# A graph-network layer: hand-overs between the engines used a step later, and the edge filter's bias added by a product

## The chip, the cores and the metric

The kernel runs on one core of one Trainium2 chip. The metric is the device time of one launch in microseconds (us); nine runs of the kernel before had a median of 5747.03 us (5734.28 to 5781.86). The core's engines each work through a queue of their own in order: TensorE (PE, with its weight loads listed as PEld), VectorE (DVE), ScalarE (ACT), GpSimd (POOL, which here issues the indirect transfers) and SyncE (SP, which issues the other transfers). They wait for one another by semaphores.

## The reference

```python
h = relu(layernorm(x))                      # 12500 nodes x 128
h = h @ W_in2f
Wij = ssp(f_ij @ W_f1 + b_f1) @ W_f2 + b_f2 # 412500 edges, f_ij has 20 columns
Wij = Wij * rcut_ij[:, None]
x_ij = h[idx_j] * Wij                       # idx_j = dst, sorted
agg = segment_sum(x_ij, idx_i)              # idx_i = src, in no order
out = x + ssp(agg @ W_o1 + b_o1) @ W_o2 + b_o2
```

`ssp` is softplus less log 2. All is in float32. The rows of `h` are gathered by the sorted index, so 512 edges after one another need few different rows; the sums go to the unsorted index.

## The kernel before

**Chunks.** The edges are cut into 806 chunks of 512 (four tiles of 128), four chunks to a group, and the groups into seven segments. For each chunk: PE makes the hidden layer `z` (L653) for a pair of chunks at a time; ACT takes |z|, Exp and Ln of it (L656, L657, L662) and DVE joins them to `r` (L668). PE multiplies `r` by W_f2 into `v` (L764), one fp32 product per tile, on top of the bias.

**The bias.** The two biases of the hidden layer and of the filter are joined once to `bf12`, the same row on all 128 partitions (`biases`, L304). For the first two chunks PE writes it into `v` by a product of one row of ones; for the others ACT copies it there (L757), and the products then add to it.

**Picking.** DVE makes a one-hot matrix `at` of a chunk's node numbers (L744), SP loads 32 rows of `h`, split in three bf16 parts, into `near` (L608), and PE's products of the two, one per tile, give the gathered rows `picked` (L772). ACT scales them by the edge weight to `hg` (L780). `v` and `picked` share three PSUM banks by the tag "v".

**Message and scatter.** DVE multiplies `v` by `hg` into `o` (L791); POOL scatters the four tiles of `o` to slots in DRAM by indirect transfers (L795).

**Slots.** To know the slots, DVE marks each edge's block of 128 source nodes (`inb`, L673), PE adds running counts in the bank `free` (L725 and L692), and DVE takes the count that belongs to each edge by a maximum, `top` (L697). From four chunks' `top` it makes slot numbers (L717 to L721), in the first group for each chunk alone.

**Collecting.** When a segment's edges are all scattered, SP reads its slots back to `m`, DVE makes a one-hot `to` of the node within the block (L844), and PE's products `acc` (L857) sum the rows, added into `agg` (L878, L880). This runs under the chunks of the next segments; the last segment is collected after the last chunk, together with the layer's end (`finish`).

**Order.** The order on each engine is written out by hand: `step(k)` issues the work around chunk k, and what a step issues stands in each engine's queue in that order. Before, step k issues on DVE `inb`, in even steps `r`, `at` for chunk k+2, then the message `o` of chunk k, the sum into `agg`, `to`, and last `top` of the count that PE makes in the same step. On PE it issues `value` for k+1, `pick` for k+1, the two count products, in even steps `z` of k+4, and the collecting products. On ACT: the bias copy for k+2, `hg` for k+1, Abs and Exp of k+4 or, in odd steps, Ln.

Of the kernel before, what the change touches and what calls it, by code (L numbers as in the profile page):

```python
# [9 lines left out]
F32 = mybir.dt.float32  # L10
BF16 = mybir.dt.bfloat16
# [6 lines left out]
P = 128  # L18
# [23 lines left out]
def gnn_kernel(  # L42
# [107 lines left out]
    turn = sbuf("turn", [P, NCHUNK, QT])  # L150
    places = sbuf("places", [P, P])
    bf12 = sbuf("bf12", [P, P])
    zero = sbuf("zero", [P, ZR * RW])
    bad = sbuf("bad", [1, NFLAG])
    none = sbuf("none", [P, 3 * P], BF16)
# [96 lines left out]
    def constants():  # L252

        early[0] = load_x(0)
        part_load(0)
        first_load(0)
        nc.sync.dma_start(win, w_in2f)

        for j in range(NCHUNK):
            nc.sync.dma_start(wf1[32 * j:32 * j + RBF, :], w_f1)  # L260

        nc.scalar.preload_act_table_set("natural_log_exp_and_others")
        nc.scalar.dma_start(bf1, b_f1[:, None])
        nc.scalar.dma_start(wf2, w_f2)
        nc.scalar.dma_start(bf2, b_f2[None, :].to_broadcast([P, P]))
        make_identity(nc, ident)
        for _ in bounds(0, nc.gpsimd):
            pass

        prow_i = early_room[:WP, rows_at + 5 * NC:rows_at + 5 * NC + 1].bitcast(I32)  # L270
        nc.gpsimd.iota(prow_i, pattern=[[0, 1]], base=0, channel_multiplier=43)
        nc.gpsimd.iota(places, pattern=[[1, P]], base=0, channel_multiplier=0,
                       allow_small_or_imprecise_dtypes=True)

        nc.gpsimd.memset(after, 1.0)
        nc.gpsimd.affine_select(out=after, in_=after, compare_op=ALU.is_ge, fill=0.0, base=-1,
                                pattern=[[1, P]], channel_multiplier=-1)
        nc.gpsimd.memset(zero, 0.0)

        nc.gpsimd.memset(before, 1.0)  # L280
        nc.gpsimd.affine_select(out=before, in_=before, compare_op=ALU.is_ge, fill=0.0, base=-1,
                                pattern=[[-1, P]], channel_multiplier=1)
        nc.gpsimd.iota(spare, pattern=[[1, 1]], base=N, channel_multiplier=1,
                       allow_small_or_imprecise_dtypes=True)
        nc.vector.memset(eps, EPS)
        nc.vector.memset(half, 0.5)
        nc.vector.memset(bad, 0.0)
        nc.vector.memset(rel[:, NPART - 1, :], 0.0)
        nc.vector.memset(ones, 1.0)
        nc.vector.memset(none, 0.0)  # L290

        for t in range(QT):
            nc.vector.memset(turn[:, :, t:t + 1], -1.0 if t % 2 else 1.0)
        nc.vector.tensor_scalar(prow_i, prow_i, 7, None, op0=ALU.logical_shift_right)
        nc.vector.tensor_copy(prow, prow_i)
        nc.vector.scalar_tensor_tensor(after, ident, BIG, after, op0=ALU.mult, op1=ALU.add)

        nc.vector.tensor_scalar(rest_of, after, -1.0, 1.0, op0=ALU.mult, op1=ALU.add)

    def biases(psum):  # L300

        nc.vector.tensor_scalar(nbf1, bf1, -1.0, None, op0=ALU.mult)
        b12 = psum.tile([P, QT, P], F32, name="b12", tag="acc")[:, 0, :]
        nc.tensor.matmul(b12, bf1.to_broadcast([P, P]), wf2, start=True, stop=True)  # L304
        nc.vector.tensor_add(bf12, b12, bf2)

    def late_loads():
        nc.sync.dma_start(wo1, w_o1)
# [85 lines left out]
        nc.scalar.activation(a, a, AF.Exp, scale=-1.0)  # L394
        nc.scalar.activation(a, a, AF.Ln, bias=half, scale=0.5)

    def finish(t0, n, sT, quad, psum):


        n0 = t0 * P  # L400
# [21 lines left out]
            xi = xo[:p, cs, :]  # L422
            nc.vector.tensor_add(xi, xi, spread(bo2[:p, :], xi.shape[1]))
        yield
        v = psum.tile([P, QT, P], F32, name="v_out", tag="v", bufs=3)
        for i in range(n):
            nc.tensor.matmul(v[:, i, :], r_n[:, i * P:(i + 1) * P], wo2, start=True, stop=True)
        yield
# [89 lines left out]
    with tc.tile_pool(name="edge", bufs=2) as edge, tc.tile_pool(  # L518
# [46 lines left out]
        class Group:  # L565
# [82 lines left out]
            def hidden(self, c):  # L648

                z = psum.tile([P, 2, CH], F32, name="z")  # L650
                for k in range(2):
                    rows = slice(32 * (c + k), 32 * (c + k) + RBF)
                    nc.tensor.matmul(z[:, k, :], wf1[rows, :], self.f[rows, :],  # L653
                                     start=True, stop=True)
                a = quad.tile([P, 2, CH], F32, name="a", bufs=2)
                nc.scalar.activation(a, z, AF.Abs, bias=bf1)  # L656
                nc.scalar.activation(a, a, AF.Exp, scale=-1.0)  # L657
                self.pair[c] = z, a

            def hidden_log(self, c):  # L660
                _, a = self.pair[c]
                nc.scalar.activation(a, a, AF.Ln, bias=half, scale=0.5)  # L662

            def hidden_end(self, c):

# [30 lines left out]
            def rank_end(self, c):  # L696
# [3 lines left out]
                if self.g * NCHUNK + c == seg.c1 - 1:  # L700
# [7 lines left out]
                    for b0, b1 in ((0, seg.b0), (seg.b0, seg.b1), (seg.b1, NBLK)):  # L708
                        i += 1
                        if b0 < b1:  # L710
                            self.limit(i + 1, ALU.is_gt, seg.tiles(b0) * P // 2,
                                       both[:, :, 0, b0:b1])
                if c == self.n - 1 or self.g == 0:

                    w = slice(c * QT if self.g == 0 else 0, (c + 1) * QT)
                    top = self.top[:, w]
                    nc.vector.scalar_tensor_tensor(top, top, -BIG,  # L717
                                                   turn.rearrange("p c t -> p (c t)")[:, w],
# [26 lines left out]
                                        op=ALU.is_equal)  # L745
                self.at_w = at

            def bias(self, c):


                v = psum.tile([P, QT, P], F32, name="v", bufs=3)
                if self.g * NCHUNK + c < 2:
                    nc.tensor.matmul(v.rearrange("p t f -> p (t f)"),
                                     ones[0:1, :].to_broadcast([1, P]), spread(bf12[0:1, :], QT),
                                     start=True, stop=False, skip_group_check=True)
                else:
                    nc.scalar.activation(v, spread(bf12, QT), AF.Copy)  # L757
                return v

            def value(self, c, v):  # L760

                r = self.pair[c // 2 * 2][:, c % 2, :]
                for i in range(QT):
                    nc.tensor.matmul(v[:, i, :], r[:, i * P:(i + 1) * P], wf2,  # L764
                                     start=False, stop=True, skip_group_check=True)
                return v

            def pick(self, c, at, ps):

                near = self.near.pop(c)  # L770
                for i in range(QT):
                    nc.tensor.matmul(ps[:, i, :], at[:, i * P:(i + 1) * P], near,  # L772
                                     start=i == 0, stop=i == QT - 1, skip_group_check=True)

            def picked(self, c, ps):

# [111 lines left out]
        def of(k):  # L888
            return groups[k // NCHUNK], k % NCHUNK

        hgs, ats, vs, bs = {}, {}, {}, {}

        summed = []
        owed = []
# [29 lines left out]
        def window(g, c):  # L924
            g.window(c)
            ats[g.g * NCHUNK + c] = g.at_w

        def group(j):
            if j not in groups and j < NG:
                groups[j] = Group(j)  # L930
# [9 lines left out]
        def step(k, units=()):  # L940

            def has(j):
                return 0 <= j < NCH

            group((k + LG) // NCHUNK)
            part("rows", min(k + LW, 2 * k + 3, NEXT if k < NEXT - 3 else NCH), rows)
            for c, u in units:
                c.load(u + AHEAD)  # L950

            part("blocks", min(k + LR + 1, 2 * k + 1), blocks)
            part("end", min(k + LZ - 2, made.get("log", -1)), pairs(hidden_end))
            part("window", k + 2 if k > 0 else k + 1, window)
            if has(k):
                g, c = of(k)
                g.message(c, vs.pop(k), hgs.pop(k))
            for c in owed:
                c.keep()
            owed.clear()  # L960
            if has(k + 1):
                g, c = of(k + 1)
                vs[k + 1] = g.value(c, bs.pop(k + 1))
                ps = psum.tile([P, QT, P], F32, name="picked", tag="v", bufs=3)
                g.pick(c, ats.pop(k + 1), ps)
            if has(k + 2):

                bs[k + 2] = of(k + 2)[0].bias(of(k + 2)[1])
            if has(k + 1):
                hgs[k + 1] = g.picked(c, ps)  # L970
            for c, u in units:
                c.compare(u)
            upto = max(made["rank"], min(k + LR, 2 * k + 1))
            ready = [ranks(j) for j in range(made["rank"] + 1, upto + 1)]
            made["rank"] = upto
            for r in ready[:1]:
                next(r, None)
            part("hidden", k + LZ, pairs(hidden))
            part("log", k + LZ - 1, pairs(hidden_log))
            for c, u in units:  # L980
                if summed:
                    summed[0].add(summed[1])
                summed[:] = c, u
            for r in ready:
                for _ in r:
                    pass

        zeros = {}
        units = {}
# [79 lines left out]
        with tc.manual_schedule():  # L1069
# [21 lines left out]
            part("rows", 1, rows)  # L1091
            biases(psum)
            part("end", 0, hidden_end)
            bs[0] = groups[0].bias(0)
            group(1)
            aside = side()
            for k in range(-1, max(NCH, max(units) + 1)):
# [22 lines left out]
            for b in range(0, NBLK, QT):  # L1120
                n = min(QT, NBLK - b)
                sT = kept["agg"][:, b:b + n, :].rearrange("p c f -> p (c f)")
                outs.append(finish(b, n, sT, quad, psum))

            def go(q):
                if 0 <= q < NQ:
# [85 lines left out]
```

## Time and profile before

| | |
|---|---|
| median of 9 runs | 5747.03 us |
| profiled execution | 5746.84 us |
| its span | 5745.1 us, 71871 instructions |
| mean granted TensorE clock | 0.721 of full |
| busy: PE, DVE, POOL, ACT | 67%, 59%, 54%, 47% |
| first scatter issued | 29.4 us after the start |
| DMA, mean over the span | 143 GB/s |

The profile is one execution. A group of instructions has its line, engine, operation, the names of what it writes and reads, its count, then its busy time and the mean length of one in ns, then the time that its engine stood idle just ahead of it and who ended most of that. "Issue" means that nothing in the profile explains the wait. fp32 products appear as two records each.

### The profile page before, as it was taken

How to read it: one execution, taken by the hardware profiler on the slowest of the kernel's cores; microseconds unless marked ns; L12 is line 12 of the kernel's file. 1: busy time of each engine (PE TensorE's matmuls, PEld its weight loads, DVE VectorE, ACT ScalarE, POOL GpSimd, SP SyncE). 2: the span in 40 equal slices, each digit the busy share in tenths (PEclk: the TensorE clock that was granted, in tenths of full speed). 3: DMA queues.
4: the chain of work that ended last, by engine and by line, in shares of the span. 5: the costliest groups of instructions: out<-in, count | busy, mean ns of one | idle time of the engine just before them, and what ended most of it. 6: DMA issues, size and time to landing. Idle time of an engine off the chain costs nothing. (4 is left out here: it accounts for less than half of the span.)

```text
span 5745.1 us, 71871 instructions
## 1 busy us (share of the span) xinstructions
PE 3848.1 (67%) x21576; PEld 2895.6 (50%) x21576; DVE 3380.4 (59%) x6726; ACT 2718.1 (47%) x5490; POOL 3101.0 (54%) x3244
## 2 busy tenths in 40 slices
PE   6555555555555555477777777777777777777668
PEld 3333333333333333356656566656666665656557
DVE  5555555555444444456665666666666666666667
ACT  4555454555444444444444444444444444444444
POOL 5555555555555555555555555555555555555550
PEclk7666566666565565678877777787787777777889
DMA  5444444343333333255664554655555556545447
GB/s 151 138 135 142 130 126 133 116 132 106 101 90 91 100 106 93 81 147 162 184 192 139 155 157 146 192 166 162 151 170 183 160 151 181 168 141 148 141 131 219
DMA packets 515581, 820.80 MB, mean 143 GB/s; under 512 B 177074, under 2 KB 312870, under 8 KB 515186
## 3 DMA queue, kind: packets, MB, share of 16 engines
q1 hardware_dynamic: 411586, 602.85, 36.9%
q0 software_dynamic: 103168, 213.15, 11.3%
q8 instruction: 176, 2.88, 0.2%
q14 instruction: 219, 1.79, 0.1%
q10 hardware_dynamic: 432, 0.13, 0.0%
HBM read 419.09 MB, written 396.64 MB: 142 GB/s over the span
## 5 line engine op out<-in xcount | busy, mean ns | idle before, releaser
L795 POOL DMA_INDIRECT slots<-o,slot x3224 | 3097.9, 961 | 2503.6 <-DVE o L791 1600.4
L764 PE MATMUL v<-wf,r 128*128 128x128 f32 x6448 | 1203.6, 345 | 539.2 <-issue 229.3
L857 PEld LDWEIGHTS acc<-to,m 128*128 128x128 f32 x8132 | 1232.2, 235 | 579.1 <-issue 311.7
L857 PE MATMUL acc<-to,m 128*128 128x128 f32 x8132 | 1324.6, 326 | 281.2 <-DVE agg L880 133.9
L764 PEld LDWEIGHTS v<-wf,r 128*128 128x128 f32 x6448 | 1079.3, 252 | 847.4 <-issue 335.4
L780 ACT ACTIVATE hg<-picked,rcut 128x128 f32<-128x128 f32 x3224 | 913.3, 365 | 1213.3 <-remote 835.7
L697 DVE TENSOR_REDUCE top<-free 128x4 f32<-128x392 f32 x806 | 451.9, 561 | 1587.8 <-remote 942.8
L757 ACT ACTIVATE v<-bf 128x512 f32<-128x512 f32 x804 | 478.1, 595 | 1230.4 <-DVE o L791 902.7
L653 PE MATMUL z<-f,wf 20*128 20x512 f32 x1612 | 654.7, 867 | 404.2 <-DVE r L668 241.3
L844 DVE TENSOR_TENSOR to<-count_ps,m 128x512 f32<-128x512 f32 (+3 forms) x824 | 644.5, 806 | 281.3 <-remote 98.0
L772 PE MATMUL picked<-near,at 96*128 96x128 bf16 x3224 | 398.4, 256 | 470.5 <-ACT hg L780 273.0
L668 DVE SCALAR_TENSOR_TENSOR r<-z,nbf,a 128x1024 f32<-128x1024 f32 x403 | 516.3, 1281 | 238.7 <-ACT a L662 124.8
L656 ACT ACTIVATE a<-z,bf 128x1024 f32<-128x1024 f32 x403 | 454.0, 1127 | 403.7 <-remote 294.5
L772 PEld LDWEIGHTS <-at 96*128 96x128 bf16 x3224 | 313.4, 118 | 533.1 <-issue 506.1
L791 DVE TENSOR_TENSOR o<-v,hg 128x512 f32<-128x512 f32 x806 | 548.5, 680 | 15.5 <-ACT hg L780 8.7
L744 DVE TENSOR_TENSOR at<-count_ps,rel 96x512 bf16<-96x512 f32 x806 | 545.8, 677 | 0.0
L653 PEld LDWEIGHTS z<-f,wf 20*128 20x128 f32 x1612 | 173.8, 238 | 620.7 <-issue 381.9
L662 ACT ACTIVATE a<-a,half 128x1024 f32<-128x1024 f32 x403 | 468.1, 1162 | 0.0
L673 DVE TENSOR_TENSOR inb<-count_ps,blk 128x392 f16<-128x392 f32 x806 | 446.5, 555 | 0.0
L657 ACT ACTIVATE a<-a 128x1024 f32<-128x1024 f32 x403 | 426.2, 1057 | 12.8
L725 PE MATMUL free<-inb,rest_of 128*128 128x392 f16 x806 | 334.9, 416 | 129.3 <-issue 47.9
L692 PE MATMUL free<-inb,after 128*128 128x392 f16 x806 | 335.3, 416 | 17.6 <-issue 12.6
(108 smaller groups left out, 1145.5 us busy)
## 6 DMA issues: line engine op xcount, KB each, us to landing
m<-slots SPq DMA_DIRECT2D x311, 387.0 KB
m<-slots SPq DMA_DIRECT2D x317, 258.0 KB
rel<-rel_d SPq DMA_DIRECT2D x202, 384.0 KB
m<-slots SPq DMA_DIRECT2D x172, 322.5 KB
slots<-o,slot POOLq DMA_INDIRECT x3224
slots<-zero SPq DMA_DIRECT2D x96, 387.0 KB
slots<-zero SPq DMA_DIRECT2D x64, 516.0 KB
f<-in_f_t SPq DMA_DIRECT2D x404, 80.0 KB
```

Source lines behind the costliest of these rows:

```text
L653: nc.tensor.matmul(z[:, k, :], wf1[rows, :], self.f[rows, :], start=True, stop=True)
L662: nc.scalar.activation(a, a, AF.Ln, bias=half, scale=0.5)
L668: nc.vector.scalar_tensor_tensor(r, z, nbf1, a, op0=ALU.max, op1=ALU.add)
L744: nc.vector.tensor_tensor(at, prow_ps.to_broadcast([WP, CH]), self.rel[:, c, :], op=ALU.is_equal)
L757: nc.scalar.activation(v, spread(bf12, QT), AF.Copy)
L764: nc.tensor.matmul(v[:, i, :], r[:, i * P:(i + 1) * P], wf2, start=False, stop=True, skip_group_check=True)
L772: nc.tensor.matmul(ps[:, i, :], at[:, i * P:(i + 1) * P], near, start=i == 0, stop=i == QT - 1, skip_group_check=True)
L780: nc.scalar.activation(hg[:, i, :], ps[:, i, :], AF.Copy, scale=self.rcut[:, j:j + 1])
L791: nc.vector.tensor_mul(o[:, :, :P], v, hg)
L795: put = nc.gpsimd.indirect_dma_start(out=views[j % VIEWS], out_offset=bass.IndirectOffsetOnAxis(ap=self.slot[:, j:j + 1], axis=0), in_=o[: ...
L844: nc.vector.tensor_tensor(to[:, :n, :], count_ps[:, None, :].to_broadcast([P, n, P]), self.m[u][:, :n, P:].to_broadcast([P, n, P]), op=ALU ...
L857: nc.tensor.matmul(self.acc[b // QT][:, i, :], m[:, j, :P], to[:, j, :], start=t == 0, stop=t == self.seg.tiles(b) - 1)
```

## The change

- `message(k)` moves to the front of the step; `top` follows it, of the count that PE made a step earlier; `inb`, `r`, and `at` (for k+3) come after.
- `pick` runs two chunks ahead, into two banks of its own (tag "picked"), and stands ahead of `value` on PE. `hg` for k+1 reads what was picked in the step before.
- `v` has one bank. Its bias is no longer copied in by ACT: after the four products a fifth adds it, 128 rows of ones in bf16 by a matrix `bf12_p` whose first three rows are the bias split into three bf16 parts (`bias_parts`) and whose other rows are zero.
- Abs, Exp and Ln of the hidden layer are issued together, a step after `z`.
- In the first ten steps the order is another one, and the counts gain their lead more slowly: `min(k + 6, k + 1 + (k + 1) // 2)` in place of `min(k + 6, 2k + 1)`. The first three groups, not one, get slot numbers chunk by chunk.
- `finish` spreads its outputs over the tags "picked" and "v".

```diff
+        nc.gpsimd.memset(ones_b, 1.0)
+        nc.gpsimd.memset(bf12_p, 0.0)
...
+    def bias_parts():
+        left = bf12[:3, :]
+        for k in range(3):
+            part = ln.tile([3, P], BF16, name="bias_part", bufs=1)
+            nc.vector.tensor_copy(part, left)
+            nc.vector.scalar_tensor_tensor(bf12_p[:3, :], part, ident[:3, k:k + 1],
+                                           bf12_p[:3, :], op0=ALU.mult, op1=ALU.add)
+            if k < 2:
+                nc.vector.tensor_sub(left, left, part)
...
+                self.pair[c] = z
+
+            def hidden_log(self, c):
+                z = self.pair[c]
                 a = quad.tile([P, 2, CH], F32, name="a", bufs=2)
                 nc.scalar.activation(a, z, AF.Abs, bias=bf1)
                 nc.scalar.activation(a, a, AF.Exp, scale=-1.0)
+                nc.scalar.activation(a, a, AF.Ln, bias=half, scale=0.5)
                 self.pair[c] = z, a
-
-            def hidden_log(self, c):
-                _, a = self.pair[c]
-                nc.scalar.activation(a, a, AF.Ln, bias=half, scale=0.5)
...
-                if c == self.n - 1 or self.g == 0:
+                if c == self.n - 1 or self.g < 3:
...
-            def bias(self, c):
-                v = psum.tile([P, QT, P], F32, name="v", bufs=3)
...
-                    nc.scalar.activation(v, spread(bf12, QT), AF.Copy)
-                return v
-
-            def value(self, c, v):
+            def value(self, c):
+                v = psum.tile([P, QT, P], F32, name="v", bufs=1)
                 r = self.pair[c // 2 * 2][:, c % 2, :]
                 for i in range(QT):
                     nc.tensor.matmul(v[:, i, :], r[:, i * P:(i + 1) * P], wf2,
-                                     start=False, stop=True, skip_group_check=True)
+                                     start=i == 0, stop=False, skip_group_check=True)
+                nc.tensor.matmul(v.rearrange("p t f -> p (t f)"), ones_b, spread(bf12_p, QT),
+                                 start=False, stop=True, skip_group_check=True)
                 return v
-            def pick(self, c, at, ps):
+            def pick(self, c, at):
+                ps = psum.tile([P, QT, P], F32, name="picked", bufs=2)
...
-            part("blocks", min(k + LR + 1, 2 * k + 1), blocks)
-            part("end", min(k + LZ - 2, made.get("log", -1)), pairs(hidden_end))
-            part("window", k + 2 if k > 0 else k + 1, window)
+            def slots():
+                for r in ranked:
+                    next(r, None)
+                ranked.clear()
+
+            if not steady:
+                slots()
             if has(k):
                 g, c = of(k)
                 g.message(c, vs.pop(k), hgs.pop(k))
+            if steady:
+                slots()
             for c in owed:
                 c.keep()
             owed.clear()
+            if not steady:
+                part("window", k + 1 if k < 1 else k + 2 if k < 6 else k + 3, window)
+            part("blocks", made["rank"] + 2, blocks)
+            part("end", min(k + LZ - 2, made["log"]), pairs(hidden_end))
+            if steady:
+                part("window", k + 3, window)
+
+            part("pick", k + 1 if k < 8 else k + 2, pick)
             if has(k + 1):
                 g, c = of(k + 1)
-                vs[k + 1] = g.value(c, bs.pop(k + 1))
-                ps = psum.tile([P, QT, P], F32, name="picked", tag="v", bufs=3)
-                g.pick(c, ats.pop(k + 1), ps)
-            if has(k + 2):
-                bs[k + 2] = of(k + 2)[0].bias(of(k + 2)[1])
+                vs[k + 1] = g.value(c)
+
             if has(k + 1):
-                hgs[k + 1] = g.picked(c, ps)
+                hgs[k + 1] = g.picked(c, ps.pop(k + 1))
+            part("log", min(k + LZ - 1, made["hidden"]), pairs(hidden_log))
+
             for c, u in units:
                 c.compare(u)
-            upto = max(made["rank"], min(k + LR, 2 * k + 1))
-            ready = [ranks(j) for j in range(made["rank"] + 1, upto + 1)]
+            upto = max(made["rank"], min(k + LR, k + 1 + (k + 1) // 2))
+            for j in range(made["rank"] + 1, min(upto, NCH - 1) + 1):
+                slots()
+                ranked.append(ranks(j))
+                next(ranked[0])
             made["rank"] = upto
-            for r in ready[:1]:
-                next(r, None)
             part("hidden", k + LZ, pairs(hidden))
-            part("log", k + LZ - 1, pairs(hidden_log))
+            if k < 4:
+                part("log", k + LZ, pairs(hidden_log))
             for c, u in units:
                 if summed:
                     summed[0].add(summed[1])
                 summed[:] = c, u
-            for r in ready:
-                for _ in r:
-                    pass
...
+                tag = ("picked", 2) if b // QT % 3 else ("v", 1)
+                outs.append(finish(b, n, sT, quad, psum, *tag))
```

## The prediction

> **What bounds the kernel now.** I read the page's busy shares first, then its groups, then the waits, two stages of the windows, and last the timeline of one stretch. The page's chain that ended last holds only the final instruction here, so it names no path. No engine is near full:
>
> ```profile
> PE 3848.1 (67%) x21576; PEld 2895.6 (50%) x21576; DVE 3380.4 (59%) x6726; ACT 2718.1 (47%) x5490; POOL 3101.0 (54%) x3244
> ...
> L795 POOL DMA_INDIRECT slots<-o,slot x3224 | 3097.9, 961 | 2503.6 <-DVE o L791 1600.4
> L697 DVE TENSOR_REDUCE top<-free 128x4 f32<-128x392 f32 x806 | 451.9, 561 | 1587.8 <-remote 942.8
> L757 ACT ACTIVATE v<-bf 128x512 f32<-128x512 f32 x804 | 478.1, 595 | 1230.4 <-DVE o L791 902.7
> L725 PE MATMUL free<-inb,rest_of 128*128 128x392 f16 x806 | 334.9, 416 | 129.3 <-issue 47.9
> ```
>
> The span, 5745.1 us, is 806 chunks of 7.13 us. In a chunk POOL issues four scatters; it waits for the product `o` (L791) 1600 us in all. So the hand-overs among PE, ACT and DVE that lead to `o` set the pace. The waits (total, times, longest, in us) say where they are late:
>
> ```profile
> POOL slots L795 <- DVE o L791: 1600.4, 364, 25.4
> DVE top L697 <- remote: 942.8, 152, 11.7
> ACT v L757 <- DVE o L791: 902.7, 328, 8.7
> POOL slots L795 <- issue: 882.7, 2803, 1.8
> ACT hg L780 <- remote: 835.7, 162, 9.6
> ```
>
> DVE stops at the count's maximum `top` (L697), which stands ahead of the next `o` in its queue, for 1587.8 us. ACT stops at the bias copy (L757), which waits for `o` to free a bank of `v`, and ahead of `hg` (L780), which the next `o` needs. "Remote" is a release that the profile gives to no instruction. The timeline shows one (start, length, in brackets the idle time before):
>
> ```profile
> 1499.56 0.68 DVE L791 TENSOR_TENSOR o<-v,hg 128x512 f32<-128x512 f32 x1
> ...
> 1501.08 2.08 PE L764 MATMUL v<-wf,r 128*128 128x128 f32 x8
> ...
> 1508.11 1.14 ACT L780 ACTIVATE hg<-picked,rcut 128x128 f32<-128x128 f32 x4 [7.24 <-remote]
> 1508.15 0.57 DVE L697 TENSOR_REDUCE top<-free 128x4 f32<-128x392 f32 x1 [7.92 <-remote]
> ...
> 1508.63 0.56 DVE L673 TENSOR_TENSOR inb<-count_ps,blk 128x392 f16<-128x392 f32 x1
> 1509.11 0.68 DVE L744 TENSOR_TENSOR at<-count_ps,rel 96x512 bf16<-96x512 f32 x1
> ...
> 1509.70 0.68 DVE L791 TENSOR_TENSOR o<-v,hg 128x512 f32<-128x512 f32 x1
> ...
> 1510.66 0.96 POOL L795 DMA_INDIRECT slots<-o,slot  x1 [5.08 <-DVE o L791]
> ```
>
> ACT and DVE both stand still for 7 us and go on at the same moment, 5 us after PE's last product on record ended. I call this a pause; 152 of them are on DVE. Their cause is not in the profile. After one, DVE does `top`, `inb` and `at` before `o`. The stages differ in PE's work, hardly in pace (columns: PE, PEld, DVE, ACT, POOL busy, PE clock, DMA share, GB/s):
>
> ```profile
> 1000.00:2000.00 1000.00, 551.98 (x2464) 357.21 (x2464) 495.28 (x1072) 489.29 (x1002) 569.36 (x593) 0.61 0.37 105
> 3000.00:4000.00 1000.00, 763.05 (x4662) 611.81 (x4659) 619.72 (x1144) 463.63 (x934) 541.83 (x564) 0.79 0.53 158
> ```
>
> 593 and 564 scatters are 148 and 141 chunks, so 6.75 us a chunk without collecting and 7.09 with it.
>
> **The bias, by ACT before, by PE now.** ACT loses 804 copies of 0.595 us, 478 us of busy time; ACT is 47% busy, so what counts is that `hg` no longer stands behind a wait for `o`. PE gains 806 products of 128x512 with their weight loads. No such product is in the trace. The nearest row is L725, 392 columns in 0.416 us, so 512/392 x 0.416 = 0.54 us and 438 us in all. The Trainium skill ("TensorE: Matmul & The Clock Gate", Part 1) times a matmul of 512 columns at 427 ns on the half clock and 216 ns on the full one; at this trace's mean clock of 0.721 that makes an estimate of about 0.30 us and 240 us. I take the row, 438 us. Most of it lies in PE's idle third: PE has 5745 - 3848 = 1897 us free. It is on the path only where `o` waits for `v`; I charge one in five, +88 us (bounds 0 and +438).
>
> **Picking two chunks ahead, two banks.** `picked` had one bank in practice (PE waited 273.0 us at L772 for `hg`) and was read by ACT in the step that filled it. Now `hg`(k+1) reads what PE picked a step earlier. The four picks (0.256 us each) are neither more nor fewer; they go ahead of `value` in PE's queue, and the transfers of `near` are released and needed one step earlier alike. SP's queue of loads, which stands behind those releases, goes a step earlier with them. No cost.
>
> **`o` ahead of `top`, `inb`, `at`; counts a step later.** The message is now DVE's first work in a step, and `top` reads the product of the step before. Of the 1587.8 us at `top`, 942.8 are pauses and 645 are ordinary lateness of PE. With a whole step to hide it, the 645 could go altogether or, if DVE then waits at `o` for `v` instead, not at all; I take half, -322 us. After a pause `o` no longer stands behind `top` 0.56, `inb` 0.56, `at` 0.68 and, in every second step, `r` 1.28 (L668): 2.44 us on average, 152 x 2.44 = 371 us. Part of that was needed for `hg` anyway (1.14 us), and the late work has to be done before the next stop; I take half, -185 us (bounds 0 and -371). The pauses themselves I leave.
>
> **`v` with one bank.** This adds a wait: `value`(k+1) on PE waits for `o`(k) on DVE. Behind it in PE's queue stand the bias product, both count products, z and the collecting products; DVE waits for the counts a step later and for `v`. The loop is `o` 0.68, four products 1.1 to 2.1 us (the 2.08 above is the half clock), bias 0.54: at most 3.3 us against 7.1, and the rest of DVE's step (3380.4/806 - 0.68 = 3.5 us) lies beside it. Nothing more is charged, but this is where the slower rival sits. Here a rule speaks against the change: the same page, "A second HAM failure mode: psum-queue depth-cycling", says that PE idling briefly between groups as it cycles through PSUM banks makes the clock swing to half. The row (clock 0.61 where PE works 0.55 of the time, 0.79 where 0.76) says that more work brings more clock. By the row the collecting stage needs 763.05/141 = 5.41 us of PE a chunk, with bias (0.50 at that clock) 5.91; by the rule, with the clock back at 0.61, 5.91 x 0.79/0.61 = 7.65.
>
> **Small parts.** Abs and Exp join Ln a step later: the same three instructions of 1.13, 1.06 and 1.16 us, still due two steps after z; 0. Splitting the bias: eight DVE operations on 3 rows at about 0.2 us (the smallest rows here take 0.16 to 0.29), two memsets; +2 us before the first scatter at 29.4 us. Slot numbers by chunk in two more groups: six more sets of three at 0.17 us, +3 us at most, and the slower ramp of counts hides it; 0. The finish keeps three banks under two names; 0.
>
> **Sum.** 5745 - 322 - 185 + 88 + 2 = 5328, and 1.7 us around the span: 5330 us. The profiled execution took 5746.84, the median is 5747.03, so no correction.
>
> **Rivals.**
> (a) All of it is hidden, pauses partly too. POOL's floor is 4 x (0.961 + 882.7/2803) = 5.1 us a chunk; PE's in the collecting stages 5.91. With 352 chunks ahead of these (1408 scatters of the first segment) at 5.1 and 454 at 5.91, plus 29 us before and 140 after the scatters: 1795 + 2683 + 169 = 4647. Half way between this and my forecast is about 4990. For it: POOL follows `o` at once, every earlier `o` is an earlier scatter. Against: the pauses.
> (b) PE becomes the bound, slower. Place: `value` waiting for the one bank of `v`, with the bias product behind. Price: at a clock of 0.61, 7.65 instead of 7.09 us over 454 chunks, +254 us, 6000. It decides from where 5.91 x 0.79/clock passes 7.09: a clock under 0.66 in the collecting stages. For it: PE already has the most work and gets 11% more. Against: PE idles a third of the span.
> (c) The pace is set by the pauses and by nothing that the change touches: 6.75 and 7.09 us in stages with 38% more PE work speak for it. The lateness at `top` just moves to `o`: about 5747, 5650 to 5800. Against: the 1.8 us of DVE work between a pause's end and `o`.
>
> **How the numbers follow.** Forecast 0.48 (5100 to 5600), (a) 0.16, (b) 0.26, (c) 0.10. A change of 0.3% is about what a measurement of this kernel can tell from none. (c) falls to faster, within and slower as 0.04, 0.04, 0.02; so faster 0.68, same 0.04, slower 0.28. The range goes from 4800, inside (a), to 5950, inside (b), and leaves out about 0.06 below and 0.13 above.
>
> **What the profile after would show.** Right: the group of `v<-bf` on ACT is gone; idle time ahead of `top` well under 1000 us and none of it moved to `o`; POOL waiting for `o` 1100 to 1200 us; PE's busy time up by 240 to 440 us; chunks of about 6.5 us. Wrong: `o` waiting for PE `v` for hundreds of us, PE waiting for `o` at `value`, or a clock under 0.66 after 3000 us (rival b); pauses as many and longer, with the idle time now in front of `o` (rival c).

## The result and the profile after

| | before | after |
|---|---|---|
| median | 5745.47 us (31 runs, 5695.65 to 5781.86) | 5264.94 us (10 runs, 5254.64 to 5277.04) |
| after / before | | 0.9167 [0.9149, 0.9186] |
| span of the profiled execution | 5745.1 us | 5256.9 us |
| mean PE clock | 0.721 | 0.799 |
| chunk (scatters from first to last, over 806) | 6.92 us | 6.31 us |
| after the last scatter | 140 us | 142 us |

The changed kernel takes 8.3% less time; the forecast was 5330 us. The page of after, its busy shares and its groups:

```profile
PE 3831.6 (73%) x22378; PEld 2820.5 (54%) x22378; DVE 3378.1 (64%) x6752; ACT 2331.9 (44%) x4686; POOL 3098.1 (59%) x3246
...
L804 POOL DMA_INDIRECT slots<-o,slot x3224 | 3094.6, 960 | 2016.2 <-DVE o L800 1124.6
L769 PE MATMUL v<-wf,r 128*128 128x128 f32 x6448 | 1219.2, 348 | 831.9 <-DVE o L800 767.4
L800 DVE TENSOR_TENSOR o<-v,hg 128x512 f32<-128x512 f32 x806 | 552.8, 686 | 1271.1 <-remote 771.7
L713 DVE TENSOR_REDUCE top<-free 128x4 f32<-128x392 f32 x806 | 448.3, 556 | 81.8 <-remote 49.5
L771 PE MATMUL v<-bf_p,ones_b 128*128 128x512 bf16 x806 | 388.8, 482 | 0.7 <-issue 0.7
```

POOL's scatters cost the same as before; the idle time ahead of them fell from 2503.6 to 2016.2 us. That is 487.4 us, and the span fell by 488.2: the whole gain lies there, 475.8 of it in POOL's waits for `o` (1600.4 to 1124.6). On DVE the idle time did not leave, it changed places: 1587.8 us ahead of `top` became 1271.1 ahead of `o`. And PE now waits 767.4 us for `o` at `value`, which it did not do before. The waits of after (total, times, longest, in us) show the pauses still there, in front of `o` and `hg`:

```profile
POOL slots L804 <- DVE o L800: 1124.6, 420, 21.9
POOL slots L804 <- issue: 870.1, 2762, 1.2
DVE o L800 <- remote: 771.7, 191, 9.1
PE v L769 <- DVE o L800: 767.4, 303, 9.4
ACT hg L789 <- remote: 403.8, 86, 9.8
```

`o` with 191 such waits and `top` before with 152 are one row each. DVE has more of them, before and then after:

```profile
DVE agg L880 <- remote: 115.2, 19, 8.3
...
DVE to L844 <- remote: 98.0, 23, 6.9
```

```profile
DVE to L853 <- remote: 78.6, 25, 5.0
...
DVE agg L889 <- remote: 62.8, 11, 7.7
...
DVE top L713 <- remote: 49.5, 38, 5.7
```

In all, "remote" stops DVE 194 times for 1156.0 us before and 266 times for 968.9 us after (one of 6.3 us is not shown). The stops are not fewer, but in sum a sixth shorter. What differs most is what follows a pause. The timeline of after (start, length, idle time before in brackets) at one of them:

```profile
1511.52 0.96 POOL L804 DMA_INDIRECT slots<-o,slot  x1 [0.30 <-issue]
1513.85 0.69 DVE L800 TENSOR_TENSOR o<-v,hg 128x512 f32<-128x512 f32 x1 [4.61 <-remote]
1514.50 0.57 DVE L713 TENSOR_REDUCE top<-free 128x4 f32<-128x392 f32 x1
...
1514.56 1.11 ACT L675 ACTIVATE a<-z,bf 128x1024 f32<-128x1024 f32 x1 [6.75 <-remote]
...
1514.60 2.08 PE L769 MATMUL v<-wf,r 128*128 128x128 f32 x8 [4.43 <-DVE o L800]
1514.82 0.96 POOL L804 DMA_INDIRECT slots<-o,slot  x1 [2.35 <-DVE o L800]
```

When DVE and ACT go on, `o` is the first thing DVE does, its `hg` lies ready, and POOL scatters 0.97 us later after 2.35 us of idleness. In the stretch of before, shown with the prediction, DVE had to do `top`, `inb` and `at` and ACT `hg` first: the scatter came 2.55 us after ACT went on, and POOL had been idle for 5.08 us.

Counted over all pauses: I took every stretch of more than 3 us between the first scatter and the last in which neither ACT nor DVE works, and kept those at whose end POOL stands idle or is on the last scatter that it has. Before has 151 of them; POOL is then idle 6.22 us at each, 938 us in all, and the next scatter comes 5.05 us after the engines go on. After has 119, with 3.01 us each, 358 us in all, and a scatter after 1.57 us. Nearly all of the difference lies behind the pauses: the ways from their ends to the next scatter sum to 763 us before and 186 after. What counts as a pause matters for the size: with stretches of more than 2 us the idleness is 1043 us before and 593 after, and those ways 838 and 335. POOL's other waiting for `o` goes from 664 to 774 us with the one limit and from 559 to 540 with the other. So the gain is a shorter way from a pause's end to the next scatter, some 500 us, and the ordinary lateness did not shrink clearly.

The windows of after (columns as in the prediction) answer to those of before:

```profile
1000.00:2000.00 1000.00, 632.88 (x2848) 402.38 (x2849) 532.58 (x1128) 459.12 (x934) 631.24 (x658) 0.67 0.41 116
3000.00:4000.00 1000.00, 799.21 (x5250) 632.93 (x5250) 690.00 (x1296) 428.94 (x859) 591.80 (x619) 0.89 0.60 180
```

658 and 619 scatters are 164.5 and 154.75 chunks, 6.08 and 6.46 us each (6.75 and 7.09 before). PE spends 799.21/154.75 = 5.16 us a chunk in the second window, less than the 5.41 of before although it makes the bias product too; the clock there went from 0.79 to 0.89.

### The profile page after: what moved, and what is told of

The parts are those of the page before. It is cut to its first block, busy times and chain, and to the rows that moved or that the text cites. A ratio compares the mean times of both kernels' runs of the same rounds, so it can differ in the third digit from the quotient of the medians.

```text
span 5256.9 us, 73728 instructions
## 1 busy us (share of the span) xinstructions
PE 3831.6 (73%) x22378; PEld 2820.5 (54%) x22378; DVE 3378.1 (64%) x6752; ACT 2331.9 (44%) x4686; POOL 3098.1 (59%) x3246
## 5 line engine op out<-in xcount | busy, mean ns | idle before, releaser
L804 POOL DMA_INDIRECT slots<-o,slot x3224 | 3094.6, 960 | 2016.2 <-DVE o L800 1124.6
L769 PE MATMUL v<-wf,r 128*128 128x128 f32 x6448 | 1219.2, 348 | 831.9 <-DVE o L800 767.4
L769 PEld LDWEIGHTS v<-wf,r 128*128 128x128 f32 x6448 | 1056.0, 248 | 913.5 <-DVE o L800 809.8
L789 ACT ACTIVATE hg<-picked,rcut 128x128 f32<-128x128 f32 x3224 | 902.2, 369 | 1202.5 <-remote 403.8
L800 DVE TENSOR_TENSOR o<-v,hg 128x512 f32<-128x512 f32 x806 | 552.8, 686 | 1271.1 <-remote 771.7
L866 PEld LDWEIGHTS acc<-to,m 128*128 128x128 f32 x8132 | 1103.5, 212 | 464.2 <-issue 339.0
L866 PE MATMUL acc<-to,m 128*128 128x128 f32 x8132 | 1196.3, 302 | 210.6 <-issue 139.0
L668 PE MATMUL z<-f,wf 20*128 20x512 f32 x1612 | 579.0, 800 | 208.9 <-DVE r L684 129.7
L713 DVE TENSOR_REDUCE top<-free 128x4 f32<-128x392 f32 x806 | 448.3, 556 | 81.8 <-remote 49.5
L780 PEld LDWEIGHTS <-at 96*128 96x128 bf16 x3224 | 277.0, 112 | 373.8 <-issue 238.2
L780 PE MATMUL picked<-near,at 96*128 96x128 bf16 x3224 | 378.9, 246 | 105.0 <-issue 49.3
L771 PE MATMUL v<-bf_p,ones_b 128*128 128x512 bf16 x806 | 388.8, 482 | 0.7 <-issue 0.7
L668 PEld LDWEIGHTS z<-f,wf 20*128 20x128 f32 x1612 | 151.0, 228 | 410.4 <-issue 206.5
```

Of the source, the lines that this page charges most:

```text
L769: nc.tensor.matmul(v[:, i, :], r[:, i * P:(i + 1) * P], wf2, start=i == 0, stop=False, skip_group_check=True)
L789: nc.scalar.activation(hg[:, i, :], ps[:, i, :], AF.Copy, scale=self.rcut[:, j:j + 1])
L800: nc.vector.tensor_mul(o[:, :, :P], v, hg)
L804: put = nc.gpsimd.indirect_dma_start(out=views[j % VIEWS], out_offset=bass.IndirectOffsetOnAxis(ap=self.slot[:, j:j + 1], axis=0), in_=o[: ...
L866: nc.tensor.matmul(self.acc[b // QT][:, i, :], m[:, j, :P], to[:, j, :], start=t == 0, stop=t == self.seg.tiles(b) - 1)
```

## The experiments

The experiments fell on two different conditions of the chip. Beside the first four kernels below the kernel before took 4229.39 us, beside the next four 4227.64, not 5750, and none of the traces of these eight shows a wait for "remote". Beside the last four it took 5751.27 and 5756.74 us. One chip showed both at different times, so no run here tells what decides it. Each time stands beside that of the kernel before from the same chip and time. The 8.3% belong to the condition with pauses; the other shows what the change is worth without them. The expectations of the first four were written for the condition with pauses, so their microseconds can't be compared with what was measured, only their order.

### Without pauses

**The bias alone.** The kernel before, with the bias added by a product:

```diff
+                v = psum.tile([P, QT, P], F32, name="v", bufs=2)
...
-                                     start=False, stop=True, skip_group_check=True)
+                                     start=i == 0, stop=False, skip_group_check=True)
+                nc.tensor.matmul(v.rearrange("p t f -> p (t f)"), ones_b, spread(bf12_p, QT),
+                                 start=False, stop=True, skip_group_check=True)
...
-                vs[k + 1] = g.value(c, bs.pop(k + 1))
...
-                ps = psum.tile([P, QT, P], F32, name="picked", tag="v", bufs=3)
+                vs[k + 1] = g.value(c)
+                ps = psum.tile([P, QT, P], F32, name="picked", bufs=1)
...
-                bs[k + 2] = of(k + 2)[0].bias(of(k + 2)[1])
```

> The kernel before with one part of the change: the bias by a product on PE, v in two banks and picked in one. If the gain came from taking ACT's wait for o (902.7 us) away, this takes most of the way from 5745 to 5265, about 5400. If it came from the order (o ahead of top and a step for every hand-over), it does little: 5650 to 5750, and DVE still stops at top for over 1300 us. If the product is a cost on PE's path, about 5800.

Measured: 4229.43 us beside 4229.39, ratio 1.0001 [0.9991, 1.0011]. The waits of this kernel:

```profile
ACT hg L798 <- PE picked L790: 1229.6, 642, 8.8
POOL slots L813 <- issue: 788.4, 2585, 0.3
...
POOL slots L813 <- DVE o L809: 47.7, 67, 25.3
```

POOL almost never waits for `o`: 3224 scatters of 0.961 us and the 0.305 us between two (788.4/2585) make 4082 us of the 4227.3 us span; what is left is the start and the end. Moving 478 us of ACT's work to PE is worth nothing here, since POOL is the bound, and 1229.6 us of waiting on ACT cost nothing either.

**The order alone.** The kernel before with the message first in a step and `top` a step later, the bias still on ACT:

```diff
+            steady = k >= 10
...
                 g.message(c, vs.pop(k), hgs.pop(k))
+            slots()
...
+            if steady:
+                part("blocks", min(k + LR + 1, 2 * k + 1), blocks)
+                part("end", min(k + LZ - 2, made.get("log", -1)), pairs(hidden_end))
+                part("window", k + 2, window)
...
+            if k >= 9:
+                ranked.extend(ready)
```

> The kernel before with another part alone: from step 10 on the message stands first on DVE, top reads the count of the step before, and inb, r and at come after; the bias stays on ACT. By the prediction's terms for this order (-322 and -185 us) about 5240 to 5450. If ACT's bias copy, which waits for o and stands ahead of hg, holds the loop, there is little gain: 5600 to 5750, the idle time going from top to o.

Measured: 4321.06 beside 4229.39, ratio 1.0218 [1.0199, 1.0238]. By itself the order is 2.2% slower. POOL's waits for `o` are three times the 47.7 us of the run with the bias alone, and `o` now waits for this step's own rows:

```profile
POOL slots L795 <- DVE o L791: 142.7, 110, 25.7
```

```profile
L791 DVE TENSOR_TENSOR o<-v,hg 128x512 f32<-128x512 f32 x806 | 549.4, 682 | 223.4 <-ACT hg L780 220.7
L697 DVE TENSOR_REDUCE top<-free 128x4 f32<-128x392 f32 x806 | 445.2, 552 | 5.3 <-PE free L692 5.3
```

The idle time of `top` is gone here as in the kernel after, and stands in front of `o`.

**Order and bias together**, the two edits above in one kernel:

> Both parts on the kernel before: bias by a product with two banks for v, and the message first; picking still one chunk ahead with one bank. If picking ahead is worth nothing, about 5265 as the whole change; if v's one bank costs the change something (PE waits 767 us for o there), even below, 5150. If hg's wait for the pick of the same step holds the loop, 5400 to 5600.

Measured: 4307.9, ratio 1.0182 [1.0165, 1.0199]. The bias product takes at most some 0.4% off the cost of the order (1.0218 to 1.0182; the intervals touch).

**All of the change but the picking.** The kernel after, picking one chunk ahead again:

```diff
-            part("pick", k + 1 if k < 8 else k + 2, pick)
+            part("pick", k + 1, pick)
...
-                v = psum.tile([P, QT, P], F32, name="v", bufs=1)
+                v = psum.tile([P, QT, P], F32, name="v", bufs=2)
...
-                ps = psum.tile([P, QT, P], F32, name="picked", bufs=2)
+                ps = psum.tile([P, QT, P], F32, name="picked", bufs=1)
```

> The changed kernel with picking one chunk ahead again and the banks the other way round, v two and picked one; all else as changed. It should stand near the run with order and bias: 5150 to 5300 if the one bank of v is what holds the changed kernel, 5350 to 5600 if the second bank of picked is what made the gain.

Measured: 4303.3, ratio 1.0174 [1.0157, 1.0191], the same as order and bias together. So the slower ramp of the counts, the joined Abs, Exp and Ln, the slot numbers by chunk, `at` a step earlier and the pick ahead of `value` add nothing here that shows. ACT's wait is the one that picking ahead is to take away:

```profile
ACT hg L789 <- PE picked L780: 1569.2, 357, 11.3
```

**The kernel after, unchanged.**

> The changed kernel itself, unchanged, beside the one before on one chip. In the four runs above the kernel before took 4229 us, not 5745, and no wait in their traces is given to remote. If the change gains by doing with the pauses, its ratio depends on them: with them 0.917 (5265 to 5745), without them near the runs of its parts, 1.00 to 1.03. If the gain came from the hand-overs as such, the ratio is 0.92 on either.

Measured: 4246.23 beside 4227.64, ratio 1.0039 [1.0025, 1.0053]: 0.4% slower. Its waits:

```profile
POOL slots L804 <- issue: 764.2, 2506, 0.3
...
PE v L769 <- DVE o L800: 529.5, 245, 6.9
...
ACT hg L789 <- PE picked L780: 281.8, 145, 6.8
...
POOL slots L804 <- DVE o L800: 63.6, 81, 22.0
```

Against the run without picking ahead, ACT's wait for `picked` fell from 1569.2 to 281.8 us and the ratio from 1.0174 to 1.0039. Picking two ahead, with the second bank that it needs, is thus what pays for the order; the two were not tried apart. Little more is to be won here: POOL waits 63.6 us for `o` in all. Of the 19 us lost, 15 seem to lie at the end: 131 us pass after the last scatter, 116 in the run with the bias alone. What in the layer's end makes that was not tried.

**`o` last.** The kernel after with `top`, `inb`, `r` and `at` ahead of the message again:

```diff
+            if steady:
+                slots()
+                part("blocks", made["rank"] + 2, blocks)
+                part("end", min(k + LZ - 2, made["log"]), pairs(hidden_end))
+                part("window", k + 3, window)
             if has(k):
...
                 g.message(c, vs.pop(k), hgs.pop(k))
-            if steady:
-                slots()
```

> The changed kernel with the message o again behind top, inb, r and at on DVE; top still reads the count of the step before, picking still two ahead. With pauses, the term of the prediction for this (-185 us, bounds 0 and -371) says 150 to 400 us above the changed kernel. Without pauses POOL is never short of o for long, and it makes under 50 us, or even gains, since at and inb come earlier for PE.

Measured: 5206.72 beside 4227.64, ratio 1.2329 [1.229, 1.2368]. This missed by far. The waits:

```profile
DVE top L713 <- PE free L708: 1363.1, 699, 4.3
...
PE v L769 <- DVE o L800: 1210.2, 469, 6.6
POOL slots L804 <- DVE o L800: 1082.6, 564, 21.6
```

With one bank for `v`, `value` waits for `o`; the counts stand behind `value` on PE; `top` waits for the counts; and `o` stands behind `top` on DVE. The ring is closed once per chunk, and POOL is no longer the bound. With `o` in front, the ring is open. The waits fit this reading; the rival, that `o` behind the others is slow with any number of banks, is answered in part by the first experiment, in which `o` stands behind `inb`, `r` and `at` too, `v` has two banks and the time is 4229.43 us. So the order and the single bank belong together: here the bank can be spared only because `o` stands first.

**`top` last.** The kernel after with `slots()` moved from behind the message to the end of the step:

```diff
-            if steady:
-                slots()
...
+            if steady:
+                slots()
```

> The changed kernel with top read in the same step as its count is made, last on DVE, as before; o still first. With pauses, the prediction's term for the lateness at top (-322 us, bounds 0 and -645) says 200 to 400 us above the changed kernel. Without pauses under 60 us either way.

Measured: 4275.56, ratio 1.0120 [1.0091, 1.0150]. The step's delay of the counts is worth 0.7% against the kernel after (4275.56 to 4246.23); `top` then waits for `free`, for which it waits 7.7 us in all in the kernel after:

```profile
DVE top L713 <- PE free L708: 470.0, 338, 4.1
```

**Two banks for `v`.** To free a PSUM bank, the constants of DVE's comparisons (`inb`, `at`, `to`) are read from SBUF instead of PSUM, two edits at once:

```diff
-        count_ps, prow_ps = counts[:, :P], counts[:WP, P:]
+        count_ps, prow_ps = places, prow
...
-                v = psum.tile([P, QT, P], F32, name="v", bufs=1)
+                v = psum.tile([P, QT, P], F32, name="v", bufs=2)
```

> The changed kernel with two banks for v: the numbers 0 to 127 that DVE compares with (places, prow) are read from SBUF and not from a PSUM bank, which makes room. If the wait of PE for o at v (767.4 us in the changed kernel's trace) is on the path, faster than the changed kernel by 150 to 400 us with pauses; if POOL's scatters are held up by DVE's reading from SBUF, slower, POOL's mean over 961 ns.

Measured: 4843.44, ratio 1.1477 [1.1439, 1.1515]. The page of the kernel after without pauses, then of this one:

```profile
L804 POOL DMA_INDIRECT slots<-o,slot x3224 | 3094.0, 960 | 1022.4 <-issue 764.2
```

```profile
L803 POOL DMA_INDIRECT slots<-o,slot x3224 | 3705.9, 1149 | 1009.5 <-issue 799.8
L768 PE MATMUL v<-wf,r 128*128 128x128 f32 x6448 | 1087.1, 321 | 0.0
```

PE's wait at `value` is gone (529.5 to 0.0 us), but PE now waits 578.0 us for `top` ahead of the count product instead, and the second bank brings nothing that can be seen. Against the kernel after the time rose by 597 us, and the scatters alone, 1149 ns instead of 960, by 3705.9 - 3094.0 = 611.9. That leaves some 15 us that the bank could have given beside slower scatters. The constants' new place spoilt the run as a test of the bank; what it shows of the scatters is told at the end.

### With pauses

**A stop of PE put in.** In every fourth chunk PE is made to wait for two transfers one after the other (the kernel before; then the same in the kernel after):

```diff
+                if (self.g * NCHUNK + c) % 4 == 0:
+                    t = [quad.tile([P, 1], BF16, name=f"stop{i}", bufs=2) for i in range(3)]
+                    nc.scalar.activation(t[0], z[:, 0, 0:1], AF.Copy)
+                    nc.scalar.dma_start(t[1], t[0])
+                    nc.scalar.dma_start(t[2], t[1])
+                    nc.tensor.matmul(z[:, 0, 0:1], none[:, :P], t[2], start=False, stop=True,
+                                     skip_group_check=True)
```

> The kernel before with PE made to stand still in every fourth chunk: after z of that chunk ACT copies one column out, two transfers of it follow one another, and a product of zeros with what they bring must be added to z before PE goes on (it changes no number). This stands in for the pauses where a chip shows none of itself. On a chip with 4228 us for the kernel before: if hand-overs of the same step cannot do with a stop of 4 to 5 us, about 202 x 3 to 5 us more, 4850 to 5250. If POOL stays the bound anyway, under 4400.

> The changed kernel with the same stop. If its step of distance between the engines is what gained where there are pauses, it stays 200 to 500 us below the kernel before with the stop, 4350 to 4900, although without a stop it is not faster. If the gain has to do with something else in the pauses, the two kernels with the stop stand as without, within 60 us of one another.

Both were expected for a chip without pauses and fell on one with them, so the stops come on top of the pauses. Measured: 6460.18 and 5948.31 us beside 5751.27, ratios 1.1231 [1.1174, 1.1288] and 1.0325 [1.0273, 1.0377]. The waits of the kernel before with stops, then of the kernel after with stops:

```profile
POOL slots L802 <- DVE o L798: 2333.3, 356, 31.6
...
PE z L660 <- DMA stop<-stop: 1848.0, 185, 18.4
```

```profile
POOL slots L811 <- DVE o L807: 1844.7, 474, 28.2
...
PE z L675 <- DMA stop<-stop: 1146.4, 151, 18.5
```

The stops cost 6460 - 5751 = 709 us in the one and 5948 - 5265 = 683 in the other (5265 is the result above, measured beside 5745): 202 stops, 3.5 and 3.4 us each. The gap between the kernels stays as it was (5948.31/6460.18 = 0.921, against 0.917 without stops). So no sign shows that the change helps against a stop of PE itself: it seems to have no more slack than before for products that come late. That fits the count of the first section, by which it shortens the restart after pauses, in which PE's products were already on record.

**The bias alone, once more**, the kernel of the first experiment:

> The bias product alone on the kernel before, a second time, since its first run fell where there are no pauses. Beside a kernel before of 5750 (pauses): about 5400 if ACT's wait for o made the pace there, 5650 to 5800 if the order on DVE did. Beside one of 4228 (no pauses): 4228 again, POOL being the bound.

Measured: 5744.08 beside 5756.74, ratio 0.9987 [0.9966, 1.0007]. The waits:

```profile
POOL slots L813 <- DVE o L809: 1587.0, 361, 25.1
ACT hg L798 <- remote: 1300.3, 198, 13.2
DVE top L712 <- remote: 1002.6, 155, 13.8
```

ACT no longer stops ahead of `hg` for a bank of `v`, and half of those 902.7 us has become a wait for "remote" at `hg` (835.7 to 1300.3 us). POOL's waits for `o` did not change. By the count of the first section (3 us) it has 154 pauses at which POOL stands idle, 6.32 us each, and 4.83 us from a pause's end to the next scatter: like the kernel before. So the gain comes from the rest of the change. That it is the order and the picking ahead is argued from the stretches shown; with pauses neither of them, nor any of the small parts, was run alone.

**Half the scatters.** The kernel after with two of a chunk's four scatters left out, and the collecting loads reading `other`, a view of the edge features, in place of the slots:

```diff
-                for i in range(QT):
+                for i in range(QT // 2):
...
-                    self.seg.table[r:r + nb * T * P, :]
+                    other[r:r + nb * T * P, :]
```

> The changed kernel with only two of each chunk's four scatters, and with the collecting loads reading as many rows of the edge features in place of the slots. POOL then needs 2.5 us a chunk. Where there are no pauses: DVE and PE bound, 3600 to 4000. Where there are pauses: if POOL's indirect transfers make them, few are left, under 4400; if they come from elsewhere, as many as in the changed kernel, over 4800.

Measured: 3731.48 beside 5756.74, ratio 0.6482 [0.6465, 0.6499]. The waits, and the page's busy shares:

```profile
POOL slots L804 <- DVE o L800: 1755.1, 711, 21.8
...
DVE o L800 <- remote: 9.6, 17, 1.9
```

```profile
PE 3193.6 (86%) x22378; PEld 2440.3 (65%) x22378; DVE 3345.5 (90%) x6752; ACT 2320.2 (62%) x4686; POOL 1554.5 (42%) x1634
```

On the chip and at the time at which the kernel before took 5757 us, the pauses are all but gone: "remote" stands for 9.6 us at `o`, not 771.7. They depend on the scatters, or on the loads of the slots, for both were changed at once. DVE, 90% busy, is next when POOL is not in the way.

No kernel here is the fastest in both conditions: with pauses it is the kernel after, of the complete ones that were run there, without them the kernel before and the one with the bias alone.

## Why the prediction was right, and where its sum was not

5330 us was forecast and 5264.94 measured, in the likeliest case's range. The pauses, and `o` behind three or four instructions after each, were named as a place of gain, and the gain is there. That the sum came so near is luck in part: a gain of 322 us that did not come and a cost of 88 that did not come stand against a gain at the pauses that was about 500 us and not 185.

- **Lateness at `top`, -322 us: wrong.** It gave nothing. The prediction named the other bound itself, that DVE then waits at `o` for `v`, and that is what happened: POOL's waits for `o` outside the pauses did not shrink clearly (664 to 774 us or 559 to 540, by what counts as a pause), and the idle time at `top` moved to `o` (1271.1 us).
- **After a pause, -185 us: right in its mechanism, far too small.** I took the four DVE instructions, 2.44 us, times 152, and then half. By the counts POOL's idleness at pauses fell by 450 to 580 us, and its whole idle time by 487.4. The way from the pause's end to the scatter became 3.5 us shorter (5.05 to 1.57), more than DVE's four instructions. The 152 pauses of the prediction are those at `top`; DVE has 194 such waits in all. In the stretches shown `hg` is off that way as well: it ran after the pause in before (1.14 us) and lay ready in after. The sum had taken it for something that stays.
- **The bias on PE, +88 us: nothing.** The product takes 482 ns (0.54 estimated), 388.8 us of PE's time, and PE's busy time nevertheless fell by 16.5 us: at the higher clock other products took less (`z` 867 to 800 ns, `acc` 326 to 302). With the bias alone the time changed by -0.13% [-0.34, +0.07] with pauses and by 0.01% [-0.09, +0.11] without.
- **Picking ahead at no cost: right**, and more than that: without pauses it is what makes the new order bearable (1.0174 without it, 1.0039 with it).
- **`v` with one bank at no further charge: right, but not for the reason given.** The prediction's loop was 3.3 us against 7.1. It is the place of `o` that keeps it short: with `o` last and the same bank the kernel is 23% slower than the one before (without pauses).
- **Clock.** The clock rose: 0.721 to 0.799 over the span, 0.79 to 0.89 while collecting; and from 0.721 to 0.756 with the bias product alone. The row's rule, more work and more clock, held, and rival (b) lost its price. The Trainium skill ("TensorE: Matmul & The Clock Gate", "A second HAM failure mode: psum-queue depth-cycling") would have PE's short waits between groups pull the clock down. That loss did not come, but the case for it did not arise either: PE waits 767.4 us at the one bank, yet its idle time as a whole fell from 1897 to 1425 us (span less busy time). So no run here speaks against the page.

Of the signs: the group of `v<-bf` is gone, `top` idles 81.8 us, POOL waits 1124.6 us for `o`, a chunk takes 6.52 us of the span; all as forecast. PE's busy time did not rise, and the idle time at `top` did move to `o`. "PE waiting for `o` at `value`", meant as a sign of rival (b), came true (767.4 us) in a faster kernel: a wait that a shared bank causes says nothing by itself, as long as POOL's next `o` does not stand behind it. Rival (c) was half right: the pauses stayed, in sum a sixth shorter on DVE, and now stand ahead of `o`. Rival (a)'s floor of POOL, 5.1 us a chunk, is reached where there are no pauses (5.07 and 5.08 us from the first scatter to the last), by the kernel with the bias alone as by the kernel after.

## What to carry to other kernels

When several engines stop now and then together, and none is full, ask what each has still to do between the end of a stop and the next work of the engine that sets the pace; put that work first in its queues and have its inputs made a step earlier. Idle time that leaves one row must be looked for in the others before it is booked as a gain: read the idle time of the engine that sets the pace, here POOL's 487.4 us, which accounted for the whole. Run the kernel before beside every experiment, for what an order is worth can change its sign with the condition of the chip (0.917 with pauses, 1.004 without).

## What was not expected of the hardware

- **The pauses come and go with no change to the kernel.** The same kernel before took 4228 to 4229 us at two times and 5745 to 5757 at others, and one chip showed both. With pauses, DVE has 1156 us of waits that nothing on record ends; without, the eight traces have none. They nearly vanish with half the scatters (9.6 us). The traces tell a little more of "remote". All 420 such waits of ACT and DVE before ended with a change of the semaphore by which PE signals, half of them more than 3.6 us after the last product on record that signals there. In the stretch shown with the prediction that semaphore changed six times between 1508.03 and 1508.31 us and not once on record in the 12 us before, though six products that signal there had ended by 1503.16. So in a pause, as far as this record goes, PE's signals arrive late and together. This record is not whole (3056 of the semaphore's 3664 changes), and the ends of products are modelled, so whether the product or the signal is late, and why, stays open.
- **A scatter is slower when DVE reads both operands from SBUF.** With the constants of three comparisons in SBUF instead of PSUM, the comparisons took as long as in the kernel after (`inb` 554 and 556 ns), but a scatter's issue rose from 960 to 1149 ns. It is the comparisons and not the second bank: the 1402 scatters during which no comparison ran took 959 ns, the other 1822 took 1296; in the kernel after both kinds took 959 to 961. The Trainium skill ("SBUF — State Buffer", "SBUF: two separate sides") says that a DVE instruction with two SBUF inputs and a GpSimd instruction that reads SBUF lock each other out. The run agrees with it for one side: POOL's scatters grew, by 189 ns on average, while DVE's comparisons did not.
- **With work added to PE its granted clock rose** (0.721 to 0.756), so that it cost nearly nothing: 364.9 us of bias products alone made PE busy only 40 us longer (3848.1 to 3888.4).
